# A two-layer graph attention kernel: more rows summed on TensorE in layer 1, another order of the tiles, and layer 2's weights made earlier

## The chip, the cores and the metric

The kernel runs on one core of a Trainium2 chip. The metric is the device time of one execution in microseconds (us). The profile was taken of one execution on the chip. The engines are called PE (matrix products), PEld (its weight loads), DVE (vector), ACT (scalar functions), POOL (which also issues the gathers) and SP (which issues plain transfers).

## The reference

10,000 nodes with 768 features, 160,000 random edges (each in both directions, from 80,000 pairs) and 10,000 loops in the edge list; the attention adds a loop to every node once more. All numbers are fp32.

```python
def gat_conv(x, edge_index, W, a_src, a_dst, bias, heads, out_ch, concat):
    ei = _add_self_loops(edge_index, n); src, dst = ei
    xl = (x @ W).reshape(n, heads, out_ch)
    alpha_src = einsum('nhc,hc->nh', xl, a_src); alpha_dst = einsum('nhc,hc->nh', xl, a_dst)
    e = leaky_relu(alpha_src[src] + alpha_dst[dst], 0.2)
    alpha = softmax of e over the edges of one dst
    out = segment_sum(xl[src] * alpha[:, :, None], dst) + bias

h  = relu(layer_norm(gat_conv(x, W1, 4 heads of 256))) + x @ Wr1 + br1
h2 = layer_norm(gat_conv(h, W2, 1 head of 768)) + h @ Wr2 + br2
return plain_layer_norm(x + h2)
```

## The kernel before

**First stage.** All nodes go through `x @ W1` in 79 tiles of 128, and the rows, with the two logit terms of each head behind them, are written to a table in DRAM (1032 numbers a row). Beside it `prepare()` sorts the nodes by their in-degree and writes, for every sorted tile, lists of source nodes: `slots` has one column for each (tile, in-edge number). A tile has as many columns, called rows here, as its largest node may need. `slot_counts` fixes these numbers ahead: 8, 9 and 10 rows for one tile each, 11 and 12 for three each, 13 (5 tiles), 14 (6), 15 (8), 16 (7), 17 (8), 18 (7), 19 (7), 20 (6), 21 (4), 22 (4), 23 (2), 24 (2), 25, 26, 27 and 41 for one each: 1377 rows in all. `FIRST[t]` is a tile's first column. Both layers take the tiles from the smallest to the largest.

**Layer 1** (`ordered_layer1`). POOL gathers table rows into a ring of 28 (L409; one gather brings one row for each of 128 nodes, 528 KB). It works through its queue in program order, and a gather into a ring slot waits for all readers of that slot. `weights_of(t)` makes a tile's softmax weights e in two steps: logits, maximum and exponential (L454 to L462), then normalisation (L469 to L475) and the sum of the tile's first two rows on PE: ACT multiplies the identity with a column of e (L681, four diagonals a row, one for each head) and PE multiplies these with the ring row into the PSUM tile `acc` (L686). The steps are called while the tile in front has three and two rows to go. The remaining rows are summed by DVE into `acc`: of four rows, three are multiplied by ACT in the ring (L481) and added in one instruction (L488), and one is done as four products (L492).

While tile t's rows are summed, the tile before it is finished: statistics of the mean (L534, L536), ACT's root (L538), the norm and relu into h (L547, L550, L739), transposes of h (L556, copied by L559), a store of h for layer 2, and the products `xT @ Wr1` and `hT @ W2` on PE (both L162). The row of layer 2's table is copied by ACT (L704) one tile later and scattered by POOL (L706). A tile that doesn't fit in the ring (41 rows) goes through `attend_parts`: three groups with a running maximum, on DVE and ACT, the mean going to an SBUF tile `means`.

**Layer 2** (`ordered_layer2`) has a ring of 40 rows of 770 numbers (394 KB a gather). DVE sums columns 0 to 511 of every row (L492), PE columns 512 to 767 with one diagonal a row (L836, L837). PE also makes the residual of the next tile (L846, L848). Weights of the next tile are made while this one has three rows to go; the PE sums are issued at the start of their own tile, into a PSUM bank of their own. After the two norms ACT writes the output tile (L884), of which there is one buffer, and POOL scatters it (L921) behind the gathers of the tile.

All engines run their instructions in the order of the program; there is no scheduler.

Of the kernel before, what the change touches and what calls it, by code (L numbers as in the profile page):

```python
# [46 lines left out]
RING2 = 40  # L47
LEAD = 3
ON_PE2 = 512
SHARE = 4  # L50
ON_PE1 = 2
# [26 lines left out]
def gnn_kernel(ctx, tc, x, x_cols, src, dst, src_col, dst_col, W1, a_src1, a_dst1, b1, g1, be1, Wr1, br1,  # L78
# [14 lines left out]
    FIRST = [sum(SLOTS[t + 1:]) for t in range(NT)]  # L93
    TOTAL = FIRST[0] + SLOTS[0]
# [379 lines left out]
    def doubled(e, t):  # L474
        nc.vector.tensor_scalar(e[:, 0], e[:, 0], loops[:, NT - 1 - t:NT - t], None, op0=OP.mult)  # L475
# [171 lines left out]
    SLOTS, FIRST = SLOTS[::-1], FIRST[::-1]  # L647

    def nodes(t):
        return order[:, NT - 1 - t:NT - t]  # L650

    def ordered_layer1():
        nonlocal ps_big
        with tc.tile_pool(name="b1", bufs=1) as pool, tc.tile_pool(name="small1", bufs=2) as small, \
# [14 lines left out]

            def weights_of(t):  # L670

                n = SLOTS[t]
                e, _ = logits(small, ring, FIRST[t], FIRST[t] + n, ring.slot(FIRST[t])[:, C1 + H1:], H1, C1)
                yield e
                normalised(small, e, H1, t)

                acc = ps_acc.tile([P, 2 * BANK], F32, name="acc")
                diagonals = pool.tile([P, ON_PE1 * H1, P], F32, name="diagonals")
                for k in range(ON_PE1):
                    for i in range(H1):  # L680
                        nc.scalar.activation(diagonals[:, k * H1 + i, :], ident, AF.Copy, scale=e[:, k, i:i + 1])  # L681
                for k in range(ON_PE1):
                    for i in range(H1):

                        c, d = i * DH1, (i + 1) * DH1
                        nc.tensor.matmul(acc[:, c:d], diagonals[:, k * H1 + i, :],  # L686
                                         ring.slot(FIRST[t] + k)[:, c:d],
                                         start=(k == 0 and c % BANK == 0),
                                         stop=(k == ON_PE1 - 1 and (d % BANK == 0 or d == C1)),
                                         skip_group_check=True)  # L690
                yield acc

            def shared(k):
                return (k - ON_PE1) % SHARE > 0
# [3 lines left out]
            ready = []  # L698

# [10 lines left out]
            for t in range(NT + 1):  # L710
                live, events, done = t < NT, [], ON_PE1
                n = SLOTS[t] if live else 0
                whole = live and n <= ring.size
                if whole and not ready:
                    ready = list(weights_of(t))

                def multiplied(upto):
                    nonlocal done
                    while whole and done < min(upto, n):
                        if shared(done):  # L720
                            multiply(ring.slot(FIRST[t] + done), e[:, done], DH1)
                        done += 1
# [3 lines left out]
                if last:  # L726
                    r, mean_rows = last
                    stats = deviation(small, pieces(mean_rows[:, :C1], BANK))
# [6 lines left out]
                multiplied(ON_PE1 + 2)  # L735
                if last:
                    h = pool.tile([P, C1], F32, name="h")
                    scaled(h, [mean_rows[:, :C1]], stats, g1_b, be1_b)
# [3 lines left out]
                multiplied(ON_PE1 + LEAD)  # L742
                if last:
                    hT = pool.tile([P, K1, P], F32, name="hT")
                    events = [(ON_PE1 + j, move) for j, move in enumerate(columns(hT, h))]
# [8 lines left out]
                if last:  # L754
                    events.append((ON_PE1 + 2, to_layer2))
# [5 lines left out]
                if live and not whole:  # L761
                    due(n)
                    acc = ps_acc.tile([P, 2 * BANK], F32, name="acc")
                    mean_rows = pool.tile([P, C1], F32, name="means")
                    ad = small.tile([P, H1], F32, name="ad")
                    nc.vector.tensor_copy(ad, ring.slot(FIRST[t])[:, C1 + H1:])
                    attend_parts(small, ring, acc, mean_rows, ad, None, H1, DH1, t)
# [4 lines left out]
                for k in range(n if whole else 0):  # L772
                    multiplied(k + 1 + LEAD)
                    if k >= n - LEAD:
                        ready += itertools.islice(ahead, 1)
                    if k >= ON_PE1:
                        weigh(acc, ring.slot(FIRST[t] + k), e[:, k], DH1, shared=shared(k))
                    ring.fetch(FIRST[t] + k + 1 + ring.size)
                    due(k)
                due(DEGREES)  # L780
                last = None
                if live:
                    last = r, acc if whole else mean_rows
# [4 lines left out]
    def ordered_layer2():  # L788
        nonlocal ps_big
        with tc.tile_pool(name="b2", bufs=1) as pool, tc.tile_pool(name="small2", bufs=2) as small, \  # L790
                tc.tile_pool(name="ps_acc2", bufs=2, space=PSUM) as ps_acc, \
                tc.tile_pool(name="ps_q2", bufs=2, space=PSUM) as ps_big, tc.manual_schedule():
# [22 lines left out]
            nc.vector.memset(ones, 1.0)  # L815
            def weights_of(t):

# [5 lines left out]
                normalised(small, e, H2, t)  # L823
                yield

            def sums(t, acc, e):


                n = SLOTS[t]
                nc.tensor.matmul(acc, ones, b2_b[0:1, ON_PE2:], start=True, stop=False)  # L830
                for k in range(n):
                    if k == n // 2:
                        yield
                    if k % G == 0:
                        diagonals = pool.tile([P, G, P], F32, name="diagonals", bufs=2)
                    nc.scalar.activation(diagonals[:, k % G, :], ident, AF.Copy, scale=e[:, k, :])  # L836
                    nc.tensor.matmul(acc, diagonals[:, k % G, :],  # L837
                                     ring.slot(FIRST[t] + k)[:, ON_PE2:C2], start=False, stop=(k == n - 1))

            def residual(t):  # L840
# [3 lines left out]
                for c in range(0, C2, BANK):  # L844
                    d = min(C2, c + BANK)
                    nc.tensor.matmul(r[:, c:d], ident, xt[:, c:d], start=True, stop=False)  # L846
                    for j in range(K1):
                        nc.tensor.matmul(r[:, c:d], hT[:, j, :], wr2[:, j, c:d], start=False,  # L848
                                         stop=(j == K1 - 1))
                return r  # L850

            ins = {t: fetch_x(t) for t in range(min(2, NT))}
            ring.fetch(RING2)
            rs = {}
            last = None
            ready = []
            assert SLOTS[0] <= ring.size and NT > 1
            for t in range(NT + 1):
                live, tail = t < NT, iter(())
                n = SLOTS[t] if live else 0  # L860
                whole = live and n <= ring.size
                if whole and not ready:
                    ready = list(weights_of(t))
                if whole:
                    e = ready[0]
                    acc = ps_acc.tile([P, BANK], F32, name="acc")
                    sum_ = ps_acc.tile([P, BANK], F32, name="sum")[:, :C2 - ON_PE2]
                    tail = sums(t, sum_, e)
                if last:
                    h, r, means = last  # L870
                    stats = deviation(small, [a for m in means for a in pieces(m, C2 - ON_PE2)])
                    next(tail, None)
                    scaled(h, means, stats, g2_b, be2_b)
                    nc.vector.tensor_add(h, h, r[:, :C2])
                    mean, inv = deviation(small, pieces(h, C2 // 2))
                    o = pool.tile([P, C2], F32, name="out")
                for _ in tail:
                    pass

                def finish():  # L880
                    nc.vector.reciprocal(inv, inv)
                    less = small.tile([P, 1], F32, name="less")
                    nc.vector.scalar_tensor_tensor(less, mean, -1.0, inv, op0=OP.mult, op1=OP.mult)
                    nc.scalar.activation(o, h, AF.Identity, bias=less, scale=inv)  # L884

                if live:
                    if not t:
                        rs[0] = residual(0)
                        q = product(brT, wr2, C2)
                    elif t + 1 < NT:  # L890
                        rs[t + 1] = residual(t + 1)
                    r = rs.pop(t)
                    h_ = parts[4 + t % 2][:, :C2]
                    if not whole:
                        if last:
                            finish()
                        ad = small.tile([P, H2], F32, name="ad")
                        nc.vector.tensor_add(ad, ring.slot(FIRST[t])[:, C2 + H2:], lift)
                        attend_parts(small, ring, h_, h_, ad, b2_b, H2, DH2, t)
                    ready = []  # L900
                    ahead = iter(())
                    if whole and t + 1 < NT and SLOTS[t + 1] + LEAD <= ring.size:
                        ahead = weights_of(t + 1)
                    for k in range(n if whole else 0):
                        if k >= n - LEAD:
                            ready += itertools.islice(ahead, 1)
                        weigh(acc, ring.slot(FIRST[t] + k), e[:, k], ON_PE2, None if k else b2_b)
                        ring.fetch(FIRST[t] + k + 1 + ring.size)
                        if last and k == 1:
                            finish()  # L910
                        if not t and k == n - LEAD:
                            nc.vector.tensor_add(be2_b, be2_b, q[:, :C2])
                            rs[1] = residual(1)
                        if t + 2 < NT and k == n // 2:
                            ins[t + 2] = fetch_x(t + 2)
                    if t + 2 < NT and t + 2 not in ins:
                        ins[t + 2] = fetch_x(t + 2)
                elif last:
                    finish()
# [275 lines left out]
```

## Time and profile before

| what | value |
|---|---|
| time, median of 3 runs | 5635.8 us (5628.9 to 5637.64) |
| the profiled execution: time, span | 5634.25 us, 5632.5 us |
| busy: PE, DVE, POOL, ACT | 4694.2, 4446.0, 3411.6, 3145.5 us |
| mean granted clock of PE | 0.918 |
| first gather of layer 1, first gather of layer 2 | 892.1 us, 3570.5 us |
| last gather of layer 2 | 5570.7 us |
| gathers of table rows | 2754, 956 ns each on POOL |
| read from and written to DRAM | 1431.1 and 146.2 MB |

Busy times overlap: several engines work at once, and none is busy for the whole span. The stages differ (first stage up to 890 us, layer 1, layer 2), so a share of the whole span says little; the tables by stretch in the prediction are read instead. For a transfer issued by POOL the page gives two times: that on POOL itself and that to landing.

### The profile page before, as it was taken

The page shows a single profiled execution, that of the slowest core. Times are in us where ns is not written, and L with a number is a line of the kernel's source. Part 1 is how long each engine was busy: PE and PEld are TensorE (multiplying, and loading weights), DVE is VectorE, ACT ScalarE, POOL GpSimd, SP SyncE. Part 2 cuts the span into 40 slices and gives each one's busy share as a digit, 9 for nine tenths or more (in the row PEclk, how much of TensorE's full clock was granted, in tenths as well). Part 3 has the DMA queues.
Part 4 walks back from the last instruction along what each step waited for, and adds up shares of the span by engine and source line. Part 5 has one row for each costly group of instructions (what it writes and reads, how often), then busy time and mean ns, then how long its engine had stood idle before and what let it go on. Part 6 is the DMA issues. An engine that isn't in the chain of part 4 may idle for free. (4 is left out here: it accounts for less than half of the span.)

```text
span 5632.5 us, 56575 instructions
## 1 busy us (share of the span) xinstructions
PE 4694.2 (83%) x14464; PEld 2762.6 (49%) x14464; DVE 4446.0 (79%) x7881; ACT 3145.5 (56%) x8061; POOL 3411.6 (61%) x3396
## 2 busy tenths in 40 slices
PE   9999997999999998888777654499988888888772
PEld 4444444555555555444444332266556565555551
DVE  5883344788999999999998888388888887877777
ACT  3433444678878888877788766144444343333331
POOL 3446455455556666655655553477777777777773
PEclk9999998999999999999988877799999999888886
DMA  4322427789998999999998876699999999999995
GB/s 155 122 98 80 93 95 263 269 299 327 327 325 324 335 341 332 333 329 326 331 336 320 309 286 225 224 315 330 331 327 332 326 333 324 325 328 330 330 327 163
DMA packets 438659, 1580.90 MB, mean 281 GB/s; under 512 B 102764, under 2 KB 106924, under 8 KB 438327
## 3 DMA queue, kind: packets, MB, share of 16 engines
q0 software_dynamic: 341344, 1400.80, 69.9%
q1 hardware_dynamic: 93168, 170.98, 9.1%
q10 hardware_dynamic: 3814, 5.39, 0.3%
q8 instruction: 122, 2.00, 0.1%
q14 instruction: 211, 1.72, 0.1%
HBM read 1431.10 MB, written 146.19 MB: 280 GB/s over the span
## 5 line engine op out<-in xcount | busy, mean ns | idle before, releaser
L409 POOL DMA_INDIRECT ring<-table,slots x2754 | 2633.6, 956 | 1452.0 <-DVE acc L492 381.5
L492 DVE SCALAR_TENSOR_TENSOR acc<-ring,e,acc 128x256 f32<-128x256 f32 (+1 forms) x2606 | 1609.2, 618 | 134.4 <-PE acc L686 54.5
L481 ACT ACTIVATE ring<-ring,e 128x256 f32<-128x256 f32 x3536 | 1437.1, 506 | 0.0
L488 DVE TENSOR_TENSOR acc<-acc,ring 128x1024 f32<-128x1024 f32 x884 | 1089.1, 1232 | 78.6 <-DVE acc L492 0.9
L837 PE MATMUL sum<-ring,diagonals 128*128 128x256 f32 x2672 | 698.8, 425 | 258.9 <-ACT diagonals L836 256.6
L162 PE MATMUL big<-wr,xT 128*128 128x512 f32 x1896 | 867.4, 616 | 0.7 <-ACT xT L559 0.7
L848 PE MATMUL big<-w,wr 128*128 128x512 f32 (+1 forms) x2528 | 841.0, 485 | 0.0
L162 PE MATMUL big<-w,xT 128*128 128x512 f32 x1896 | 824.8, 597 | 19.1 <-DMA w<-in_W_dram 8.7
L162 PE MATMUL big<-w,hT 128*128 128x512 f32 (+1 forms) x2528 | 833.2, 487 | 1.2 <-ACT hT L559 1.2
L837 PEld LDWEIGHTS sum<-ring,diagonals 128*128 128x128 f32 x2672 | 564.8, 215 | 392.2 <-ACT diagonals L836 296.5
L162 PEld LDWEIGHTS big<-w,hT 128*128 128x128 f32 x2528 | 479.5, 190 | 375.1 <-issue 340.1
L848 PEld LDWEIGHTS big<-w,wr 128*128 128x128 f32 x2528 | 478.4, 189 | 337.0 <-issue 303.2
L162 PEld LDWEIGHTS big<-w,xT 128*128 128x128 f32 x1896 | 362.5, 192 | 478.9 <-issue 461.2
L162 PEld LDWEIGHTS big<-wr,xT 128*128 128x128 f32 x1896 | 371.6, 200 | 441.8 <-issue 440.9
L686 PE MATMUL acc<-ring,diagonals 128*128 128x256 f32 x1248 | 336.0, 430 | 277.8 <-ACT diagonals L681 245.6
L836 ACT ACTIVATE diagonals<-ident,e 128x128 f32<-128x128 f32 x1336 | 420.1, 388 | 124.2 <-PE sum L837 123.0
L884 ACT ACTIVATE out<-wr,less,sd 128x768 f32<-128x768 f32 x79 | 81.1, 1026 | 644.1 <-DMA out_dram<-out,order 556.4
L686 PEld LDWEIGHTS acc<-ring,diagonals 128*128 128x128 f32 x1248 | 269.9, 219 | 338.2 <-ACT diagonals L681 259.9
L634 DVE TENSOR_TENSOR scr<-big,as_b 128x1024 f32<-128x1024 f32 x79 | 96.7, 1225 | 382.3 <-ACT row L631 382.3
L462 ACT ACT_TABLE_LOAD x155 | 198.9, 1283 | 311.1 <-DVE e L461 283.2
L639 POOL TENSOR_TENSOR row<-row,none 128x1024 f32<-128x1024 f32 x79 | 186.9, 2366 | 270.3 <-ACT row L631 269.8
L637 ACT ACTIVATE scr<-scr 128x256 f32<-128x256 f32 x632 | 253.5, 402 | 122.9 <-DVE scr L634 122.9
(171 smaller groups left out, 3938.4 us busy)
## 6 DMA issues: line engine op xcount, KB each, us to landing
ring<-table,slots POOLq DMA_INDIRECT x2754, 5.8
table<-row SPq DMA_DIRECT2D x79, 516.0 KB, 2.9
h_d<-hT SPq DMA_DIRECT2D x79, 512.0 KB, 7.0
wr<-h_d SPq DMA_DIRECT2D x79, 512.0 KB, 6.8
xT<-in_x_cols_dram SPq DMA_DIRECT2D x79, 384.0 KB, 4.3
w<-in_W_dram SPq DMA_DIRECT2D x6, 512.0 KB, 7.3
w<-in_W_dram SPq DMA_DIRECT2D x1, 3072.0 KB, 12.9
wr<-in_Wr_dram SPq DMA_DIRECT2D x1, 3072.0 KB
```

What stands on the lines that cost most here:

```text
L162: nc.tensor.matmul(p[:, c:e], aT[:, j, :], w[:, j, c:e], start=(j == 0), stop=(j == k - 1))
L409: nc.gpsimd.indirect_dma_start(out=to, out_offset=None, in_=table, in_offset=bass.IndirectOffsetOnAxis(ap=index, axis=0), **more)
L462: nc.scalar.activation(e, e, AF.Exp)
L481: nc.scalar.activation(row[:, s], row[:, s], AF.Copy, scale=e[:, h:h + 1])
L488: nc.vector.tensor_add(acc[:, :c], acc[:, :c], row[:, :c])
L492: nc.vector.scalar_tensor_tensor(acc[:, s], row[:, s], e[:, h:h + 1], (acc if first is None else first)[:, s], op0=OP.mult, op1=OP.add)
L637: nc.scalar.activation(m[:, s], m[:, s], AF.Copy, accum_out=row[:, C1 + i * H1 + h:C1 + i * H1 + h + 1])
L639: nc.gpsimd.tensor_add(row[:, :C1], row[:, :C1], b1_b)
L686: nc.tensor.matmul(acc[:, c:d], diagonals[:, k * H1 + i, :], ring.slot(FIRST[t] + k)[:, c:d], start=(k == 0 and c % BANK == 0), stop=(k == ...
L836: nc.scalar.activation(diagonals[:, k % G, :], ident, AF.Copy, scale=e[:, k, :])
L837: nc.tensor.matmul(acc, diagonals[:, k % G, :], ring.slot(FIRST[t] + k)[:, ON_PE2:C2], start=False, stop=(k == n - 1))
L848: nc.tensor.matmul(r[:, c:d], hT[:, j, :], wr2[:, j, c:d], start=False, stop=(j == K1 - 1))
```

## The change

- The tiles are taken in another order, `TURNS`: every second one from the smallest up to the largest, then the others down again. The sizes run 8, 10, 11, 12, ... 24, 26, 41, 27, 25, ... 11, 11, 9. Lists and first columns follow that order.
- In layer 1, PE sums `on_pe(t)` rows instead of two: (2 x rows - 15) // 5, at least 1 and at most 5. The first two at most are made where they were; the others in a third step of `weights_of`, after the statistics of the tile in front.
- The tile of 41 rows writes its mean into `acc` itself instead of into an SBUF tile.
- In layer 2 the ring has 38 rows. The next tile's logits are made at row `turn` of a tile and its normalisation and PE sums three rows later. The PE sums lie in the free part of the residual's second PSUM bank; there are three residual buffers and five buffers of four diagonals (two before), and `acc` keeps two banks.
- In layer 2 the norms of the tile in front are a generator, called at the start and after rows 3, 6 and 9; its last part is the scatter. For the 41-row tile they run in front of it.

```diff
-RING2 = 40
+RING2 = 38
+DIAGONALS = 5
-ON_PE1 = 2
+ON_PE1 = 5
...
-    FIRST = [sum(SLOTS[t + 1:]) for t in range(NT)]
-    TOTAL = FIRST[0] + SLOTS[0]
+    TURNS = list(range(NT - 1, -1, -2))
+    TURNS += sorted(set(range(NT)) - set(TURNS))
+    FIRST, TOTAL = [0] * NT, 0
+    for t in TURNS:
+        FIRST[t], TOTAL = TOTAL, TOTAL + SLOTS[t]
...
+            def on_pe(t):
+                return min(max((2 * SLOTS[t] - 15) // 5, 1), ON_PE1, SLOTS[t])
...
-                for k in range(ON_PE1):
-                    for i in range(H1):
-                        nc.scalar.activation(diagonals[:, k * H1 + i, :], ident, AF.Copy, scale=e[:, k, i:i + 1])
...
+                for lo, hi in ((0, min(m, 2)), (min(m, 2), m)):
+                    for k in range(lo, hi):
+                        for i in range(H1):
+                            nc.scalar.activation(diagonals[:, k * H1 + i, :], ident, AF.Copy,
+                                                 scale=e[:, k, i:i + 1])
+                    for k in range(lo, hi):
+                        for i in range(H1):
+                            c, d = i * DH1, (i + 1) * DH1
+                            nc.tensor.matmul(acc[:, c:d], diagonals[:, k * H1 + i, :],
+                                             ring.slot(FIRST[t] + k)[:, c:d], ...)
+                    yield acc
...
                 if last:
-                    r, mean_rows = last
-                    stats = deviation(small, pieces(mean_rows[:, :C1], BANK))
+                    r, means = last
+                    stats = deviation(small, pieces(means[:, :C1], BANK))
+                for _ in ahead:
+                    pass
...
-                    attend_parts(small, ring, acc, mean_rows, ad, None, H1, DH1, t)
+                    attend_parts(small, ring, acc, acc, ad, None, H1, DH1, t)
...
-                    if k >= n - LEAD:
+                    if n - LEAD <= k < n - LEAD + 2:
                         ready += itertools.islice(ahead, 1)
-                    if k >= ON_PE1:
+                    if k >= first:
...
-                tc.tile_pool(name="ps_q2", bufs=2, space=PSUM) as ps_big, tc.manual_schedule():
+                tc.tile_pool(name="ps_q2", bufs=3, space=PSUM) as ps_big, tc.manual_schedule():
...
                 normalised(small, e, H2, t)
+                to = rs[t][:, C2:2 * C2 - ON_PE2]
+                nc.tensor.matmul(to, ones, b2_b[0:1, ON_PE2:], start=False, stop=False, ...)
+                for k in range(n):
+                    if k % G == 0:
+                        diagonals = pool.tile([P, G, P], F32, name="diagonals", bufs=DIAGONALS)
+                    nc.scalar.activation(diagonals[:, k % G, :], ident, AF.Copy, scale=e[:, k, :])
+                    nc.tensor.matmul(to, diagonals[:, k % G, :], ring.slot(FIRST[t] + k)[:, ON_PE2:C2], ...)
                 yield
...
+            def norms(t, h, r, means):
+                stats = deviation(small, [a for m in means for a in pieces(m, C2 - ON_PE2)])
+                yield
+                scaled(h, means, stats, g2_b, be2_b)
+                nc.vector.tensor_add(h, h, r[:, :C2])
+                mean, inv = deviation(small, pieces(h, C2 // 2))
+                yield
+                nc.vector.reciprocal(inv, inv)
+                less = small.tile([P, 1], F32, name="less")
+                nc.vector.scalar_tensor_tensor(less, mean, -1.0, inv, op0=OP.mult, op1=OP.mult)
+                o = pool.tile([P, C2], F32, name="out")
+                nc.scalar.activation(o, h, AF.Identity, bias=less, scale=inv)
+                yield
+                nc.gpsimd.indirect_dma_start(out=out, ..., in_=o, ...)
...
+            rs = {0: residual(0)}
+            q = product(brT, wr2, C2)
...
+            for t in range(NT):
+                if t + 1 < NT:
+                    rs[t + 1] = residual(t + 1)
...
+                    next(last, None)
+                    ready, ahead, turn = [], iter(()), n
+                    if t + 1 < NT and SLOTS[t + 1] + LEAD <= ring.size:
+                        ahead = weights_of(t + 1)
+                        turn = min(max(n // 3, n + SLOTS[t + 1] + 2 * LEAD - ring.size), n - LEAD)
+                    for k in range(n):
+                        if k in (turn, turn + LEAD):
+                            ready += itertools.islice(ahead, 1)
+                        if k in (LEAD, 2 * LEAD, 3 * LEAD):
+                            next(last, None)
+                        weigh(acc, ring.slot(FIRST[t] + k), e[:, k], ON_PE2, None if k else b2_b)
+                        ring.fetch(FIRST[t] + k + 1 + ring.size)
...
+                    last = norms(t, h, rs[t], [acc, rs[t][:, C2:2 * C2 - ON_PE2]])
```

## The prediction

> **What bounds the kernel now.** I read the slices first, then layer 1 cut tile by tile, then the waits, then a few lines in order of time. Slices (one is 140.8 us): layer 1's attention runs from slice 7 to the middle of slice 25, layer 2's from there to the end.
>
> ```profile
> DVE  5883344788999999999998888388888887877777
> POOL 3446455455556666655655553477777777777773
> DMA  4322427789998999999998876699999999999995
> ```
>
> DVE is full in layer 1, POOL level in layer 2, DMA high in both. To see who decides I cut layer 1 where DVE's L536 (once a tile, on the tile before) starts; a stretch is then one tile's period. Columns: stretch, length, then busy time of PE, PEld, DVE, ACT, POOL, then clock, DMA share, GB/s. The first seven are layer 1 tiles of 13, 16, 18, 19, 20, 22 and 24 rows a node, the next a 19-row tile of layer 2, the last layer 2's 41-row tile.
>
> ```profile
> 1197.60:1224.50 26.90, 25.89 (x88) 15.18 (x87) 23.10 (x38) 20.92 (x50) 14.17 (x16) 1.00 0.86 304
> 1787.10:1816.90 29.80, 28.78 (x100) 17.38 (x98) 27.33 (x44) 24.03 (x57) 18.01 (x19) 1.00 0.91 330
> 2218.20:2250.70 32.50, 29.30 (x88) 16.61 (x87) 29.88 (x46) 27.19 (x66) 19.91 (x21) 0.89 0.91 334
> 2451.70:2486.20 34.50, 28.01 (x86) 15.57 (x86) 31.70 (x48) 27.13 (x65) 19.85 (x21) 0.95 0.93 329
> 2626.40:2662.40 36.00, 28.89 (x88) 17.07 (x87) 33.09 (x51) 28.83 (x69) 21.73 (x23) 0.88 0.91 331
> 3038.30:3078.50 40.20, 28.99 (x88) 17.10 (x87) 35.63 (x52) 31.99 (x78) 23.56 (x25) 0.84 0.88 322
> 3257.50:3306.10 48.60, 29.03 (x88) 17.13 (x87) 38.91 (x57) 33.62 (x81) 25.45 (x27) 0.78 0.80 288
> 4818.60:4846.40 27.80, 22.29 (x76) 15.36 (x76) 21.81 (x45) 10.21 (x25) 21.20 (x22) 0.87 0.91 318
> 5542.20:5620.30 78.10, 0.00 (x0) 0.00 (x0) 54.56 (x88) 5.23 (x10) 15.11 (x16) 0.50 0.31 87
> ```
>
> Up to 14 rows PE fills the period; from 16 on DVE does (busy plus some 2.5 us of gaps); from 22 on there is more idle, since the ring of 28 must be refilled before the next tile's logits. The waits, layer 1 (1500 to 3000 us, DVE), then layer 2 (3750 to 5500 us, POOL; total, times, longest):
>
> ```profile
> DVE e L475 <- ACT e L462: 18.1, 34, 0.8
> DVE e L454 <- DMA ring<-table,slots: 5.7, 4, 3.1
> POOL ring L409 <- issue: 99.9, 328, 0.3
> POOL ring L409 <- PE sum L837: 69.7, 225, 1.5
> ```
>
> DVE waits 18 us in 1500: layer 1 is its work. In layer 2 POOL's gaps are nearly all 0.3 us, its own step: it issues without pause, 1362 transfers in 1750 us, 1.285 us each. So a layer 2 tile costs (rows + 2) x 1.285 us whatever DVE does; 19 rows give 27.0.
>
> **What the Trainium skill says.** "Perfetto Trace Analysis", DMA Instruction — SWDGE (GPSIMD): such an instruction's profiled end is the last descriptor written, not the data moved. The trace agrees: 0.97 us on POOL, 5.3 us to landing. So POOL's rate is a limit of its own. "DMA: Bandwidth & Descriptors", Where 436 GB/s comes from, puts the ceiling near 435 GB/s; 3-us stretches of gathers alone show 420 here at share 1.03, stretches with stores 230 to 310. "TensorE: Matmul & The Clock Gate", The HAM clock gate: an idle PE falls to half clock. Here L686's halves start 0.216 us apart in the 13-row tile and near 0.43 at first after a 6 us idle in the 20-row one.
>
> **Prices.** From the timeline of the 20-row tile: a shared row on DVE is 1.31 us (3.91 for three), a row of four products 2.17 (2.06 and a gap), a diagonal on ACT 0.31 (2.45 for eight). A row on PE is four fp32 products of two halves, 8 x 0.216 = 1.73 us.
>
> **Layer 1.** The rule gives 1 row on PE up to 12 rows, 2 for 13 and 14, 3 for 15 to 17, 4 for 18 and 19, 5 from 20. In the 13-row tile PE's chain closes at 26.85 us with 2 rows, so its floor is 25.1, 26.85, 28.6, 30.3 and 32.0 us for 1 to 5. DVE loses one to three rows: 1.31 us at 16 and 17 rows, 2.6 at 18, 3.5 at 19, 4.8 at 20, 21, 23 to 25 and 27, 3.9 at 22 and 26.
>
> The rows past two are made after the next tile's statistics, so a wait is added: DVE's first product needs all of acc. Before, the order is
>
> ```profile
> 2626.63 0.29 ACT L538 ACTIVATE sd<-mv,eps 128x1 f32<-128x1 f32 x1 [1.01 <-DVE mv L536]
> 2630.63 2.06 DVE L492 SCALAR_TENSOR_TENSOR acc<-ring,e,acc 128x256 f32<-128x256 f32 x4
> 2632.79 3.91 DVE L488 TENSOR_TENSOR acc<-acc,ring 128x1024 f32<-128x1024 f32 x3
> ```
>
> 4.0 us between sd and the product, filled by h. After it ACT needs 0.7 us to the first diagonal's end, then PE 1.73 a row: done at 2.6, 4.3 and 6.1 us for 3, 4, 5 rows. Stall: 0, 0.3, 2.1 us. Behind the diagonals on ACT stand layer 2's row copy, the ring products and xT; for 5 rows the third ring row comes at 9.7 against DVE's 9.6, so that queue adds nothing more. If the first two rows still run at half clock, the stall is 3.4; if ACT and PE are early, 0. I take 2.1.
>
> Periods, before to after, times tiles: 8 to 12 rows (8 tiles), 27.2 to 25.2, with the first pair -2.4 in all: -15. 15 (8): 28.4 to 28.6, +2. 16 (7): 29.7 to 28.8, -6. 17 (8): 30.5 to 29.3, -9. 18 (7): 32.5 to 30.7, -13. 19 (7): 34.6 to 31.6, -21. 20 (6): 36.0 to 33.3, -16. 21 (4): -11. 22 (4): -7. 23 to 25 and 27 (6): -16. 26: -2. The 41-row tile doesn't use the new sums; its in-place mean costs what the copy cost. Sum -114 us. The DMA takes some back: a 19-row tile at share 0.93 of 34.5 us needs 31.1 us at 1.03, and I ask 31.6; 20 rows need 31.8 of 33.3. Rows will land later, and from 19 rows on the logits have six rows of DVE or fewer as cover, 6 x 1.53 = 9 us (1.53 is the mean of three shared rows and one of products), against a landing of 6. An estimate of 0.6 us over 28 tiles of 18 to 22 rows: +17 (between 0 and 73). Layer 1: -97.
>
> Where the largest tile stands in layer 1 changes little: it costs DVE 85.5 us anywhere. At the layer's end the last product finds PE warm: 10.5 instead of 13.3 us, -3.
>
> **Layer 2.** From the first gather (3570.5) to the end are 2062 us. POOL's 1535 transfers need 45 x 1.25 + 1490 x 1.285 = 1971 us, less 3 for two stores in the tail. Start: PE now runs residual and q before the sums, which takes an estimated 10 of the 20 us that POOL loses there. End: before, the 41-row tile comes last, DVE sums it alone (last stretch above) after ACT has waited 19 us for the output buffer, and POOL is idle for 53 us. In the middle its 66 us of DVE work, the norm of the tile in front included, stand beside 43 x 1.285 = 55 us of POOL, and the ring of 38 takes up most of the rest: 5 lost. The tail is then 11 and 9 rows: landing 5, logits and exponentials 4, 17 rows at 0.79 = 13, three norms 21, store 6: 50 us. Sum 1968 + 10 + 5 + 50 = 2033: -29 (0 to -45).
>
> In between, the early weights add a wait: at the turn DVE stands until the next tile's last row has landed, and everything it still has to free stands behind. The formula leaves six free slots, 7.7 us of POOL. The last row lands 5.3 us after its issue; then logits and the next row take 2.4, and POOL wants that slot 1.4 us later. DVE's work for 19 rows is some 24 us against POOL's 27. ACT's wait for the output buffer goes, since the store is now queued at row nine instead of at the end; the sums are made ahead. I cost this at nothing.
>
> **Sum.** -97 - 3 - 29 = -129 from the profiled execution's 5634.25 us (span 5632.5), so 5505 us; the median shown, 5635.8, is 1.5 above it, which I ignore.
>
> **Rivals.** *The DMA is the bound from 19 rows on*: those tiles keep their periods, only the smaller ones' -41 remains, with -32 elsewhere: 5561. For it: share 0.93; against: 420 GB/s in places and POOL's free gaps. *No stall at the front and no DMA loss*: 22 tiles x 2.1 = 46 and 17 more: 5442. Against it: PE has to follow sd. *The turn starves POOL* (the slower side): the landing at its longest seen (8.0, +2.7) and the exponential late by its mean wait before (137 us in 52 waits, 2.6) make DVE 5.3 late, less 1.4 of cover = 3.9 us in the 45 or so tiles where the formula and not a third of the tile sets the turn: 176 us, so 5681. It turns slower from 129/45 = 2.9 us a tile.
>
> **How the numbers follow.** Main case 0.60 (own range 5470 to 5545), DMA bound 0.17, no stall 0.12, starved POOL 0.11, of which 0.03 ends near or below the break-even. A change of 0.2%, 11 us, is about what a measurement can tell from none: within it 0.03, slower 0.08, faster 0.89. The range, 5440 to 5575, takes in both faster rivals and leaves the slow one out.
>
> **What would show it.** Layer 1: 20-row tiles near 33 us, 16-row near 29, 12-row near 25; DVE waiting some 2 us for PE's acc once a tile from 20 rows; DMA share toward 1. Layer 2: POOL's gaps still 0.3, no ACT wait for the output, the end some 50 us after the last gather. I'm wrong if POOL waits for DVE's rows after each turn, or if large tiles wait for the ring as long as they gained.

## The result and the profile after

The changed kernel takes 5583.9 us (median of 4 runs, 5572.75 to 5586.68) against 5634.7 us of the kernel before beside it: ratio 0.991, interval 0.989 to 0.9924. It is faster, by 51 us, where 129 were forecast, and 5584 lies above the range. The profiled execution's span is 5584.8 us, so the same 1 to 2 us as before lie around it.

The slices first, one being 139.6 us:

```profile
DVE  5783344888988778777899888498877776778888
POOL 2446465555655554455566553477777776777775
DMA  4322426899998887788999986699999987999996
```

DVE, full in layer 1 before (8 to 9), falls to 7 and 8 where the large tiles are now (the 14th to 19th slice, 1815 to 2650 us). DMA falls with it, to 7 and 8, and POOL doesn't rise. So the freed VectorE was not put to use there, and the transfers don't look like the limit.

The stretches answer to those shown of before, cut in the same way (now at L540): tiles of 13, 16, 18, 19, 20, 22 and 24 rows of layer 1, then layer 2's 41-row tile and the 27-row tile behind it. Columns as before: stretch, length, busy time of PE, PEld, DVE, ACT, POOL, then clock, DMA share, GB/s.

```profile
1060.50:1087.30 26.80, 25.79 (x88) 15.07 (x87) 22.82 (x37) 20.89 (x50) 13.89 (x16) 1.00 0.85 305
1371.80:1400.50 28.70, 27.70 (x96) 16.75 (x95) 26.14 (x43) 23.60 (x57) 17.15 (x18) 1.00 0.95 343
1551.30:1584.20 32.90, 29.84 (x102) 18.01 (x102) 27.49 (x44) 26.38 (x65) 18.91 (x21) 1.00 0.89 330
2749.60:2783.50 33.90, 29.86 (x99) 17.84 (x98) 28.61 (x44) 27.99 (x70) 19.82 (x22) 0.97 0.91 337
2609.10:2645.90 36.80, 32.97 (x116) 20.91 (x115) 28.67 (x44) 29.14 (x74) 20.71 (x23) 0.98 0.89 324
2448.70:2492.00 43.30, 34.09 (x114) 21.68 (x113) 32.05 (x50) 30.74 (x77) 22.88 (x25) 0.90 0.82 301
2357.90:2404.00 46.10, 33.01 (x112) 20.88 (x111) 34.45 (x52) 33.99 (x86) 24.53 (x27) 0.87 0.82 304
4526.70:4596.60 69.90, 14.92 (x36) 7.86 (x36) 56.61 (x99) 5.10 (x14) 55.38 (x48) 0.60 0.90 282
4596.60:4662.50 65.90, 31.66 (x104) 21.54 (x105) 27.34 (x51) 15.82 (x46) 30.04 (x31) 0.68 0.57 194
```

The 16-row tile gained 1.1 us, as forecast. The 20-row tile has 4.4 us less DVE work than before (28.67 against 33.09) and is no shorter (36.8 against 36.0): its DVE idles 8.1 us instead of 2.9. In the last line POOL is busy 30 of 65.9 us.

The waits name the places. First POOL in layer 1 (892 to 3540 us), one line of before, one of after; the columns are total us, times, longest:

```profile
POOL table L706 <- ACT row L704: 79.1, 37, 12.6
```

```profile
POOL table L718 <- ACT row L716: 268.0, 77, 24.1
```

Then DVE of the changed kernel in ten tiles of 20 to 25 rows (2310 to 2717 us):

```profile
DVE acc L496 <- PE acc L697: 28.9, 10, 3.9
DVE e L458 <- DMA ring<-table,slots: 27.3, 7, 5.7
```

The forecast wait for acc is there, 2.9 us a tile. The wait for the next tile's rows is as large. In the kernel before the twenty tiles of 20 to 26 rows (2590 to 3410 us) show

```profile
DVE e L454 <- DMA ring<-table,slots: 40.3, 13, 6.3
```

so it has grown from 2.0 to 2.7 us a tile, and it now stands in the tiles of 20 rows, where before there was none (2310 to 2720 us, 18 to 20 rows). Cut where layer 2's first gather starts (3540.0 us), layer 1 from its first gather gained 31 us (2678 to 2648) and layer 2 17 us (2062 to 2045).

### The profile page after: what moved, and what is told of

The parts are those of the page before. It is cut to its first block, busy times and chain, and to the rows that moved or that the text cites. A ratio compares the mean times of both kernels' runs of the same rounds, so it can differ in the third digit from the quotient of the medians.

```text
span 5584.8 us, 58282 instructions
## 1 busy us (share of the span) xinstructions
PE 4822.9 (86%) x15304; PEld 2875.9 (51%) x15304; DVE 4279.6 (77%) x7692; ACT 3140.8 (56%) x8177; POOL 3367.2 (60%) x3396
## 5 line engine op out<-in xcount | busy, mean ns | idle before, releaser
L496 DVE SCALAR_TENSOR_TENSOR acc<-ring,e,acc 128x256 f32<-128x256 f32 (+1 forms) x2486 | 1546.5, 622 | 193.0 <-PE acc L697 119.4
L485 ACT ACTIVATE ring<-ring,e 128x256 f32<-128x256 f32 x3236 | 1317.2, 505 | 0.0
L492 DVE TENSOR_TENSOR acc<-acc,ring 128x1024 f32<-128x1024 f32 x809 | 996.6, 1232 | 71.2 <-ACT ring L485 2.1
L166 PE MATMUL big<-wr,xT 128*128 128x512 f32 x1896 | 830.4, 595 | 0.7 <-ACT xT L563 0.7
L851 PE MATMUL big<-ring,diagonals 128*128 128x256 f32 x2672 | 646.6, 403 | 153.0 <-ACT diagonals L850 121.5
L697 PE MATMUL acc<-ring,diagonals 128*128 128x256 f32 x2088 | 516.6, 407 | 265.9 <-ACT diagonals L691 265.8
L851 PEld LDWEIGHTS big<-ring,diagonals 128*128 128x128 f32 x2672 | 533.5, 202 | 262.5 <-ACT diagonals L850 168.1
L697 PEld LDWEIGHTS acc<-ring,diagonals 128*128 128x128 f32 x2088 | 424.4, 206 | 351.0 <-ACT diagonals L691 253.2
L850 ACT ACTIVATE diagonals<-ident,e 128x128 f32<-128x128 f32 x1336 | 398.6, 387 | 152.8 <-DVE e L476 113.5
L542 ACT ACTIVATE sd<-mv,eps 128x1 f32<-128x1 f32 x237 | 69.8, 294 | 592.8 <-DVE mv L540 592.3
L691 ACT ACTIVATE diagonals<-ident,e 128x128 f32<-128x128 f32 x1044 | 318.9, 387 | 110.8 <-DVE e L476 110.8
```

What stands on the lines that cost most here:

```text
L166: nc.tensor.matmul(p[:, c:e], aT[:, j, :], w[:, j, c:e], start=(j == 0), stop=(j == k - 1))
L485: nc.scalar.activation(row[:, s], row[:, s], AF.Copy, scale=e[:, h:h + 1])
L492: nc.vector.tensor_add(acc[:, :c], acc[:, :c], row[:, :c])
L496: nc.vector.scalar_tensor_tensor(acc[:, s], row[:, s], e[:, h:h + 1], (acc if first is None else first)[:, s], op0=OP.mult, op1=OP.add)
L697: nc.tensor.matmul(acc[:, c:d], diagonals[:, k * H1 + i, :], ring.slot(FIRST[t] + k)[:, c:d], start=(k == 0 and c % BANK == 0), stop=(k == ...
L851: nc.tensor.matmul(to, diagonals[:, k % G, :], ring.slot(FIRST[t] + k)[:, ON_PE2:C2], start=False, stop=(k == n - 1), skip_group_check=True)
```

## What stands in front of the gathers

The start of the 20-row tile in the changed kernel, in order of time (start, length, engine and line, and in brackets the idle time before it and what ended it):

```profile
2609.34 0.30 ACT L542 ACTIVATE sd<-mv,eps 128x1 f32<-128x1 f32 x1 [0.16 <-DVE mv L540]
2609.54 3.60 ACT L691 ACTIVATE diagonals<-ident,e 128x128 f32<-128x128 f32 x12
2609.71 0.95 POOL L413 DMA_INDIRECT xt<-in_x_dram,order  x1 [0.30 <-issue]
2613.05 0.77 ACT L716 COPY row<-big 128x770 f32<-128x770 f32 x1
2614.10 1.01 POOL L718 DMA_INDIRECT table<-row,order  x1 [3.43 <-ACT row L716]
2615.41 0.98 POOL L413 DMA_INDIRECT ring<-table,slots  x1 [0.30 <-PE acc L697]
2616.49 2.06 DVE L496 SCALAR_TENSOR_TENSOR acc<-ring,e,acc 128x256 f32<-128x256 f32 x4 [3.08 <-PE acc L697]
2637.96 0.17 DVE L458 TENSOR_TENSOR e<-ring 128x16 f32<-128x16 f32 x1 [3.04 <-DMA ring<-table,slots]
```

`weights_of`'s third step puts twelve diagonals (3.6 us) on ACT right behind sd (ACT's root). The copy of layer 2's row, which stood there before, now comes behind them, and POOL's scatter of that row stands in POOL's queue ahead of the tile's gathers. So POOL waits 3.4 us with free ring slots in front of it; the rows of the next tile, 20 transfers on, land as much later, and DVE waits 3.0 us for them at the logits. **Theory Q**: this queueing, and not the transfers or the wait for acc, ate the gain of the tiles from 18 rows up. Its first rivals: the rule itself (more rows on PE make DVE wait for acc), and, for layer 2, nothing to do with either.

## Experiments

**First group: the order, the rule, the x gather.** This group fell on a chip that runs the kernel before in 5955.4 us (5931.5 to 5963.4). Most of its 320 us more lie in layer 2; the absolute times expected don't hold there, only differences within the group do.

e1 moves the row copy and the scatter in front of the diagonals:

```diff
+                if full is not None:
+                    store(t - 2)
                 for _ in ahead:
                     pass
-                if full is not None:
-                    store(t - 2)
```

> The changed kernel (5584 us) with one exchange in layer 1: the copy and scatter of layer 2's row are issued before the diagonals of the third step instead of behind them. Theory Q (the queue): the scatter stands on POOL in front of the next gathers and waits for ACT's copy behind 12 diagonals (3.6 us), so every gather of a tile of 20 rows or more starts that much later and the next tile's logits wait for their last row. Then 20-row tiles fall from 36.5 to 33 or 34 us, and the whole by 40 to 75 us, to 5510 to 5545. Rival D (the DMA is full, share 0.9 and more, landing 7.9 us in place of 6.0): the order of a queue changes nothing, 20-row tiles stay within 0.7 us of 36.5 and the time within 15 us of 5584.

e2 lets `on_pe(t)` return 2 for every tile.

> The changed kernel with two rows on PE in every tile of layer 1, as before the change; order, layer 2 and the rest as changed. It prices the part on PE by itself: layer 1's tile periods should be those of the kernel before (20 rows 36.0, 19 rows 34.6, 16 rows 29.7 us). Theory Q: layer 1 gets back what the small tiles had gained (11 to 19 rows: some 40 us) and loses what the large ones had paid (20 to 27 rows: some 15 to 20 us), so 5600 to 5615. Rival O (the order of the tiles has cost something of its own in layer 1): large tiles keep their long periods also with two rows, and the time is 5620 or more.

e3 is about the 27-row tile of layer 2 (65.9 us above). After the 41-row tile the trace shows

```profile
4603.57 0.95 POOL L413 DMA_INDIRECT wr<-in_x_dram,order  x1 [0.31 <-issue]
4608.21 2.05 PE L862 MATMUL big<-wr,ident 128*128 128x512 f32 x2 [63.69 <-DMA wr<-in_x_dram,order]
4623.64 11.92 PE L851 MATMUL big<-ring,diagonals 128*128 128x256 f32 x54
4624.61 0.94 POOL L413 DMA_INDIRECT ring<-table,slots  x1 [20.10 <-PE big L851]
4630.02 0.17 DVE L553 RECIPROCAL sd<-sd 128x1 f32<-128x1 f32 x1 [30.08 <-ACT sd L542]
```

The x gather for the tile after the next is issued in the middle of every tile but the largest, where it comes last. The residual (L862) waits for it, the sums (L851) stand behind the residual on PE, the diagonals behind the sums on ACT, sd behind the diagonals; POOL waits 20 us for ring rows that the sums haven't read. e3 issues it ahead of the largest tile's parts:

```diff
                 if not whole(t):
+                    if t + 2 < NT:
+                        ins[t + 2] = fetch_x(t + 2)
                     for _ in last:
```

> The changed kernel with one gather moved in layer 2: at the tile of 41 rows, the x rows of the tile after next are asked for before its 41 rows are worked through, not after. Theory X: in the changed kernel that gather stands last on POOL, the residual of the following tile waits for it on PE and the sums of the 27-row tile behind it, so that POOL finds no free slot for 27 us; then the 27-row tile of layer 2 falls from 66 to about 38 us and the time by 20 to 28 us, to 5556 to 5564. Rival (the tiles after the largest one are held by something else, such as the diagonals' buffers or the weights made without an earlier start): less than 10 us.

e4 is e1 and e3 together.

> Both exchanges, that of layer 1 and that of layer 2. They act in different layers, so the gains should add: theories Q and X together 5485 to 5520; with Q false and X true 5555 to 5565; with Q true and X false 5510 to 5545.

| run | median us | ratio to before | layer 1, first gather to layer 2's first | layer 2 from there | 27-row tile |
|---|---|---|---|---|---|
| e1 copy and scatter first | 5938.5 | 0.997 (0.9958 to 0.9982) | 2646.2 | 2398.8 | 63.7 |
| e2 two rows | 5983.2 | 1.0046 (1.0032 to 1.006) | 2686.7 | 2386.2 | 63.8 |
| e3 early x gather | 5982.6 | 1.0052 (1.0032 to 1.0072) | 2706.7 | 2384.8 | 47.9 |
| e4 both | 5923.8 | 0.9948 (0.9937 to 0.996) | 2645.4 | 2373.6 | 48.2 |

Layer 1 is that of the changed kernel in e3. Moving the copy takes 60 us off it (e1, e4 against e3), and without that move the new rule is 20 us slower than two rows on this chip. With two rows the 28 tiles of 18 to 22 rows take 995 us of layer 1, in the kernel before 1000, so the order costs them nothing. The early x gather takes 16 us off the 27-row tile, and e4 is 15 us shorter than e1; 20 to 28 were expected. Theory Q holds so far, but e1 moves two things at once, ACT's copy and POOL's scatter.

**Second group: which of the two, and the order of the tiles.** This group, with the changed kernel itself in it, fell on a chip like the first result's (before 5637.5 us). e6 leaves ACT as it is and only lets POOL issue the scatter later, at the row where the products of h are issued; `store` returns the scatter instead of issuing it:

```diff
-                if full is not None:
-                    store(t - 2)
+                scatter = store(t - 2) if full is not None else None
...
                     events.append((first + 2, to_layer2))
+                if scatter:
+                    events.append((first + 2, scatter))
```

> The changed kernel as it is, as the measure for the others of this group. On a chip like that of the first result 5584 us, ratio 0.991 to the kernel before. On a chip like that of the first four experiments, where layer 2 runs some 320 us longer in every kernel, the two-row kernel there (1.0046) and the one with an early x gather (1.0052) say 1.006 to 1.008.

> ACT's copy of layer 2's row stays behind the diagonals as in the changed kernel; only POOL's scatter of it is put behind the gathers of the tile's first rows. If the scatter, waiting for ACT at the head of POOL's queue, is what holds the gathers back, layer 1 gets some 60 us shorter than in the changed kernel (50 to 65), as much as from moving the copy in front of the diagonals. If the late copy does harm in some other way (in ACT's own queue, through the products or through DVE), layer 1 stays within 15 us of the changed kernel's.

> The row copy in front of the diagonals and layer 2's x gather in the middle of the 41-row tile, as in the earlier run of the two together, now beside the changed kernel on one chip: 75 us shorter than that (60 from layer 1, 15 from the 27-row tile behind the largest one), so some 5510 us or 0.978 of the kernel before on a chip like that of the first result. If the exchange only paid on the other chip, under 35 us shorter.

e8 is the changed kernel with the old order of the tiles, `TURNS = list(range(NT - 1, -1, -1))`.

> The changed kernel with the tiles in the order of the kernel before, smallest to largest. By the sum of the prediction the order is worth 28 us: with the largest tile last POOL loses some 53 us in it and ends 62 us before the program, against 32 us lost around it and a tail of 55 us in the changed kernel; so 28 us longer than the changed kernel (15 to 45). If the order gives nothing, since the stall of the tile behind the largest one eats it, within 10 us.

| run | median us | ratio to before | layer 1 | layer 2 |
|---|---|---|---|---|
| e5 changed kernel | 5582.0 | 0.9909 (0.9894 to 0.9924) | 2642.5 | 2042.6 |
| e6 scatter later | 5529.6 | 0.9813 (0.98 to 0.9826) | 2591.2 | 2044.6 |
| e7 copy first, early x | 5517.2 | 0.9788 (0.9774 to 0.9801) | 2601.4 | 2021.2 |
| e8 old order | 5583.9 | 0.9906 (0.9891 to 0.9921) | 2661.3 | 2030.9 |

e6 decides it: with the same work and the copy as late as ever, 51 us of layer 1 are back. It was POOL's queue. The scatter's wait for ACT in layer 1 (892 to 3540 us) falls to

```profile
POOL table L718 <- ACT row L716: 80.6, 5, 24.1
```

that is from 77 waits (268.0 us) to 5. Ten us more came back than by the copy in front (2601.4). e7, which has that copy and the early x gather, is 65 us shorter than e5 where 75 were expected. The rival that the DMA is the limit falls too: between 2310 and 2720 us, where much the same tiles run in both, the engines moved 317 GB/s at share 0.86 in e5 and 334 at 0.91 in e6.

e8 missed: the old order is 2 us longer, not 28. The order gives 19 us in layer 1 (the forecast had 0 there) and loses 12 in layer 2, where the 27-row tile behind the largest one waits for its x gather; with that gather early (e7) layer 2 is 10 us shorter than in the old order. With two rows in every tile the order gives layer 1 less: 9 us from the kernel before to e18 below.

**Third and fourth group: both repairs together, and what is left.** e9 is e6 with the early x gather; e10 is e2 again; e11 is e9 with the row copy in front of the diagonals as well; e12 is e9 with `ON_PE1 = 4`.

> The scatter behind the first rows' gathers, and the x gather of layer 2 in the middle of the 41-row tile. Their separate gains add up, 52 us in layer 1 (5582.0 to 5529.6) and some 24 in layer 2 (the 27-row tile behind the largest one, 65 to 41): 5506 us on a chip like the last one, and 11 us shorter than with the row copy in front of the diagonals. If the two compete for the same transfers, over 5520.

> Two rows on TensorE in every tile, the rest as in the changed kernel (no early x gather, the copy where it is). By the stretches of the kernel before and the 19 us that the order gave in layer 1, layer 1 from first gather to layer 2's first gather takes 2659 us, 17 more than in the changed kernel: 5599 us. By the other chip, where two rows were 28 us shorter than the changed rule, 5555.

> As e9, with ACT's row copy moved in front of the diagonals too. If only the place of the scatter in POOL's queue matters, within 6 us of e9. If a copy in front of the diagonals holds these back (it is 0.9 us of ACT ahead of the chain for acc), 10 us longer than e9, as the copy alone moved was 11 us longer in layer 1 than the scatter alone moved.

> As e9, with at most four rows on TensorE. Twenty tiles of 20 to 27 rows give a row of 1.3 us back to VectorE and lose the wait for acc, 2.6 us a tile in the traces of the changed kernel, down to the 0.3 us of the prediction. If VectorE with its wait is what sets these tiles, 1 us less a tile, so 20 us shorter than e9. If the arrival of ring rows sets them, the same within 6 us; if the wait for acc lies beside a wait for rows anyway, 20 us longer.

That chip ran the kernel before in 6002.5 us. e9 0.9914 (0.9897 to 0.9931), e11 0.9916 (0.99 to 0.9932), e12 0.9915 (0.9898 to 0.9932), e10 1.0012 (1.0 to 1.0023); layer 1 took 2638.9, 2644.1, 2652.9 and 2685.5 us. So once the scatter is out of the way the place of ACT's copy makes no difference that could be measured on this chip, and neither does the fifth row. The same kernels once more, with the kernel before as e16:

> Scatter behind the first gathers and early x gather, as in e9. If the two losses are the whole gap, 5506 us on a chip like that of the first result (ratio 0.977), 0.991 on a slower one. If something else is missing from the prediction's sum as well, over 5520 and 0.980.

> Two rows on TensorE in every tile, the rest as in the changed kernel. On a chip like that of the first result 5599 us by the stretches (the rule as it was built is worth 17 us); if the rule as built gives nothing there either, as on the two slower chips, 5582 or less.

> As e13 with at most four rows on TensorE. On the slower chip it was 7 us longer, not to be told from none. If VectorE and its wait for acc set the tiles on a chip like the first, 10 to 20 us shorter than e13; if the arrival of ring rows sets them or the wait lies beside it, the same within 6 us or longer.

> The kernel before itself: ratio 1.000. On a slower chip its layer 2 is to show whether POOL's step stays 1.285 us and it waits for rows to be freed (then the slowness is in the transfers), or whether the step itself is longer.

Again a slower chip (before 5956.7 us): e13 0.9932 (0.9919 to 0.9946), e14 1.0041 (1.0028 to 1.0055), e15 0.9917 (0.9904 to 0.9931), e16 1.0007. Four rows are 7 us shorter than five here and were 7 us longer on the other chip: no difference. e17 and e18 repeat e9 and e10:

> As e9 and e13. On a chip that runs the kernel before in some 5635 us: 5506 us, 0.977, if the scatter and the late x gather are the whole gap; over 5520 if not. On a slower chip 0.991 to 0.993 as there.

> As e10 and e14. On a chip that runs the kernel before in some 5635 us: 5599 us (0.993) if the rule as built is worth the 17 us that the stretches give; 5582 or less if it gives nothing as built. On a slower chip 1.001 to 1.004 as there.

This chip ran the kernel before in 5637.6 us. **e17, the changed kernel with both repairs, takes 5508.0 us, ratio 0.977 (0.9757 to 0.9784)**; e18 takes 5606.7 us, 0.9943 (0.9929 to 0.9957), so the rule as built is worth 25 us on chips of this kind (e5 against e18), and not 17; on the slower chip of the first group layer 1 lost 20 by it. e17 is faster than both kernels, and lies 3 us above the predicted time. Its 20-row tile shows the queue as it should be:

```profile
2564.56 3.60 ACT L691 ACTIVATE diagonals<-ident,e 128x128 f32<-128x128 f32 x12
2565.99 1.92 POOL L413 DMA_INDIRECT ring<-table,slots  x1 [0.30 <-PE acc L697]
2568.06 0.78 ACT L716 COPY row<-big 128x770 f32<-128x770 f32 x1
2570.48 2.06 DVE L496 SCALAR_TENSOR_TENSOR acc<-ring,e,acc 128x256 f32<-128x256 f32 x4 [2.05 <-PE acc L697]
2576.93 1.01 POOL L718 DMA_INDIRECT table<-row,order  x1 [0.30 <-issue]
2589.67 0.18 DVE L458 TENSOR_TENSOR e<-ring 128x16 f32<-128x16 f32 x1 [0.41 <-DMA ring<-table,slots]
```

The copy still ends at 4.5 us after sd, but eight gathers go out ahead of the scatter, which then finds its row ready (0.30 is POOL's own gap), and the logits wait 0.4 us instead of 3.0. This tile is one of the better ones: over the same ten tiles of 20 to 25 rows as above (now 2280 to 2666 us) the wait for ring rows falls from 27.3 to 14.4 us, so part of it stays. Layer 2's x gather and residual, early, in the same kernel:

```profile
4487.53 1.61 POOL L413 DMA_INDIRECT wr<-in_x_dram,order  x1 [0.30 <-PE big L866]
4495.45 2.04 PE L863 MATMUL big<-wr,ident 128*128 128x512 f32 x2 [5.20 <-DVE new L464]
```

and the 27-row tile takes 41.4 us instead of 65.9.

## Why the prediction was wrong, step by step

**The parts of the change, measured** on the two chips that run the kernel before in 5637.5 us: all but the rule of rows (e18) -31; the rule as built (e5 against e18) -25; the scatter moved (e6) -52; the early x gather (e17 against e6) -22. The forecast of -129 left out the last two losses; e17, which has neither, measures -130. That the two sums agree so well is partly luck: e17's layer 1 is 86 us shorter than before where 100 were forecast, its layer 2 40 where 29 were. Within layer 1 the order gives 19 us that the forecast did not have (e8), and the tiles of 23 rows and more give 5 of 18.

**The step that failed** is in the part on layer 1: "Behind the diagonals on ACT stand layer 2's row copy, the ring products and xT; for 5 rows the third ring row comes at 9.7 against DVE's 9.6, so that queue adds nothing more." The row copy was seen behind the diagonals, and only DVE was asked for as the one who waits. POOL waits for the copy too, at the scatter, and everything that POOL issues stands behind that. With the copy back at its old place in front of the diagonals layer 1 is 41 us shorter (e7), with the scatter behind the gathers 51 us (e6).

Layer 1 by classes of tiles, the periods' differences to before in us, summed over the tiles; predicted without the allowance of +17 for late rows:

| rows | predicted | changed | e17 |
|---|---|---|---|
| up to 14 | -15 | -19 | -20 |
| 15 to 17 | -13 | -14 | -14 |
| 18, 19 | -34 | -20 | -33 |
| 20 to 22 | -34 | +14 | -18 |
| 23 and more | -18 | +5 | -5 |

- Up to 17 rows the PE floor and the DVE price per row were right: PE or DVE sets these tiles, and POOL has the time to wait.
- 18 to 22 rows: right with the scatter away (-51 of -68, +17 allowed for). In the changed kernel 61 of the 68 are missing.
- The front stall of DVE was taken as 2.1 us for five rows and measured 2.9 a tile in the changed kernel, 2.6 in e17 (26.2 us in 10 waits, 2280 to 2666 us, the same ten tiles of 20 to 25 rows). Five rows apply to 21 tiles, not to the 22 of the rival without a stall, which is 2 us. On the two slower chips where it was tried the fifth row paid nothing over four.
- "Where the largest tile stands in layer 1 changes little" was off by a little: the tiles of 26, 41 and 27 rows took 184.7 us before, 192.2 after, 190.6 in e17, so the class of 23 rows and more falls short in e17 too; its other five tiles gain 11 there.
- "At the layer's end ... -3": the stretch from the last statistics to layer 2's first gather went from 30.6 to 33.2 us, so +3.

**Layer 2** was forecast at 2033 us. It took 2045, and 2022 in e17. POOL's share was right, even a bit high: its step fell from 1.285 us to 1.27 (22 us over 1490 transfers). The start lost 7 us (10 forecast), the tail is 55 us (50). The term that was mis-sized is the largest tile's, "5 lost": POOL loses 32 us around it, since the x gather of the tile after the next wasn't followed to its new place, the end of a tile in the middle of the layer instead of the layer's end. With the gather early it is 8 (POOL's waits of over 0.3 us between 4420 and 4620 us in e17).

**The waits that were to go or come.** ACT's wait for the output buffer, 526.0 us between 3750 and 5500 us before, is 75.2 after. The early weights' wait at the turn, the slower rival, didn't show; POOL's commonest lines there (3750 to 5500 us) are, as before, its own gap and short waits for PE:

```profile
POOL ring L413 <- issue: 103.4, 339, 0.4
POOL ring L413 <- PE big L851: 94.1, 204, 20.1
POOL ring L413 <- DVE acc L496: 43.8, 136, 1.6
```

The result lies 23 us from the rival "the DMA is the bound from 19 rows on", and its sign to look for came true ("large tiles wait for the ring as long as they gained"), but not its cause: much the same transfers went faster in e6.

## What to carry to other kernels

When instructions are put ahead on one engine, ask for every instruction behind them who waits for its result, on every engine, and then what stands behind that waiter in its own queue: here 3.6 us on ScalarE, counted for DVE alone, held all the gathers behind one scatter. On an engine that issues transfers, put those that wait for other engines behind those that could go at once. A step tied to a place in a loop (every tile's middle, or else its end) is to be followed for the odd tile as well when the order changes.

## What had not been expected of the hardware

Chips differ, and by stage. Of the five that served the experiments, three ran the kernel before in 5955 to 6002 us and two in some 5637.5. On one of the slower ones (e16) layer 1 of the kernel before takes 2699.5 us against 2678.4, layer 2 2362.5 against 2062. Where POOL doesn't wait, its step is the 1.25 us of the faster chips. In layer 2 PE stands before its sums for nothing that the profile shows, here 1.7 to 2.2 us in front of each of three products in a row:

```profile
4963.78 0.38 PE L837 MATMUL sum<-ring,diagonals 128*128 128x256 f32 x1 [2.06 <-issue]
4965.89 0.58 PE L837 MATMUL sum<-ring,diagonals 128*128 128x256 f32 x1 [1.73 <-issue]
4968.68 0.59 PE L837 MATMUL sum<-ring,diagonals 128*128 128x256 f32 x1 [2.21 <-issue]
```

From 4000 to 5500 us such stops before the sums are 191.6 us in 124 places, and the kernel before on the first chip has none. ACT's diagonals wait for the sums for 404.1 us instead of 103.0, and POOL for ring rows that the sums still read for 183.7 instead of 60.6. PE is not alone: DVE stands in the same microseconds, and POOL in the same 1500, both until something that the profile calls "remote" and that no trace of the faster chips has in layer 2:

```profile
4968.69 0.75 DVE L492 SCALAR_TENSOR_TENSOR acc<-ring,e,acc 128x512 f32<-128x512 f32 x1 [1.97 <-remote]
POOL ring L409 <- remote: 62.2, 29, 4.3
```

What holds these engines is open. On the slower chips the same repaired kernel gained 0.7 to 0.9% instead of 2.3%, so a gain is to be compared on one chip, and the ratio of one chip isn't that of another.
